# Dividing one 512x512 weight product into halves, once, in a two-block attention kernel

## The chip, the core and the metric

The kernel runs on one NeuronCore of a Trainium2 chip. Its engines run side by side, each with an instruction queue of its own: TensorE (PE; its weight loads are listed apart as PEld), VectorE (DVE), ScalarE (ACT), GpSimd (POOL), and SyncE (SP), which here only issues DMAs. SBUF is the working memory of 128 partitions; PSUM holds what TensorE writes. The metric is the device time of one execution in microseconds, the median of several runs.

## The reference

Eight images of 512 channels and 32x32 pixels (1024 tokens), all in float32, go through two attention blocks. What matters here is block 1:

```
xn = group_norm(x)
q, k, v = q_w @ xn, k_w @ xn, v_w @ xn          # conv1x1, with biases
attn = softmax(q^T k / sqrt(512))
out = attn @ v^T                                # tokens x channels
return x + p_w @ out                            # conv1x1, with a bias
```

Block 0 is of the same kind with eight heads of 64 channels, group norm in 32 groups and an output projection of its own.

In block 1 the attention weights act on tokens and `p_w` on channels, so the value and the output weights can be multiplied with each other first, once for all images: Z = p_w v_w, a 512x512 matrix. The kernel does this, and the same with the query and key weights (M).

## The kernel before

The kernel is written in one function, `two_attention_blocks_kernel`, and a scheduling layer places each engine's instructions; `tc.keep_in_program_order` pins an instruction to its place in the written order. `matmul` and `transpose` (L67, L70) are pinned throughout, so in the profile most TensorE work has one of these two lines. Each float32 matmul of the code is two matmul records and two weight loads in the profile.

A prologue runs once. It makes M (`product(wq, wk, "m")`), runs image 0's value, query and key products for block 0, then makes Z, then a few bias rows. After it comes the loop over images: scores, exponentials and value products of block 0 (`attention0`), the projection, and block 1 of the image before, interleaved with block 0 of the image after.

The large products already use a scheme of seven multiplications of halves in place of eight, with sums and differences of the halves made beforehand (`left_sums`, `right_sums`, `wino`). The two weight products M and Z do not: `product` multiplies 512x512 by 512x512 in 16 matmuls of 128x128 by 128x512, four for each block of 128 rows, and ScalarE copies each finished block from PSUM to SBUF. Two blocks make one pair tile, and SP stores each pair to `products["z"]` in DRAM. `prepare("z")` later reads it back in quarters, and VectorE makes the sums that block 1 uses, from image to image.

What surrounds the product, in the order of the text:

- the last products of block 0's keys for image 0 (`conv(... "k0_0")`, ended by `finish()`). VectorE combines each result at L387; the last L387 is the last thing VectorE does for it
- `keep2("m", t)`: four GpSimd operations (L306) on 128x896 elements in SBUF make further sums of M, and SP stores them (L308)
- `natural(raw_v, "v", "bc")`: 16 transposes of the value weights on TensorE, then four copies from PSUM to SBUF (L776), pinned, shared by VectorE and ScalarE: tile 0's first half on VectorE and second half on ScalarE, tile 1 the same
- `norm1.group_mean`: a tiny matmul of 4 columns, and four tiny VectorE steps (L115 to L121), two of which (L117, L119) read two tensors in SBUF
- `product(wv, raw_p, "z")`: the product of this document. ScalarE copies its blocks at L789, SP stores at L791
- `norm1.affine`: another matmul of 4 columns (tile `gvar`), which feeds VectorE and then four tiny GpSimd steps
- `bias_products`: 12 matmuls of one row, copied by VectorE (L805) and sent through DRAM
- the first scores of `attention0`: TensorE, ScalarE for the exponentials (L621), VectorE for their sums (L623, L625). The next image's tiles, loaded by SP (L209), are scaled on ScalarE (L140) after the first group of exponentials.

SBUF tiles of 128x1024 elements come from one pool of 32 buffers (`big_tile`, `pair_tile`): a new tile waits for the last use of the buffer that it takes. PSUM tiles come from three pools a, b, c of two banks each in the prologue and a pool of two for small results (`acc_tile`).

The product itself and the place that calls it:

```
L789  nc.scalar.copy(ts_[ic // 2][:, ic % 2, :], ps)
...
raw_p0 = raw("p0", 3)
wv = natural(raw_v, "v", "bc")
norm1.group_mean(acc_tile("gmean_0_1")[:, :KC])
product(wv, raw_p, "z")
norm1.affine(acc_tile("gvar_0_1")[:, :KC])
```

Of the kernel before, what the change touches and what calls it, by code (L numbers as in the profile page):

```python
# [9 lines left out]
F32 = mybir.dt.float32  # L10
I32 = mybir.dt.int32
AF = mybir.ActivationFunctionType
ALU = mybir.AluOpType
AX = mybir.AxisListType

P = 128
# [13 lines left out]
def two_attention_blocks_kernel(  # L30
# [8 lines left out]
    nc = tc.nc  # L39
    B, C, T = x.shape  # L40
    KC = C // P
# [24 lines left out]
    def matmul(*args, **kw):  # L66
        tc.keep_in_program_order(nc.tensor.matmul(*args, **kw))  # L67

    def transpose(*args):
        tc.keep_in_program_order(nc.tensor.transpose(*args))  # L70
# [14 lines left out]
    products = {n: dram.tile([C, C], F32, name=f"product_{n}") for n in "mz"}  # L85
# [90 lines left out]
    def main_path(ctx):  # L176
# [8 lines left out]
        def big_tile(name, shape=(P, T)):  # L185
            return big.tile(list(shape), F32, tag="big", name=name)

        def pair_tile(name):
            return big_tile(name, (P, 2, HT))
# [5 lines left out]
        ps_pools = []  # L195
# [11 lines left out]
        def load_x(b, c, what):  # L207
            t = big_tile(f"{what}_{b}_{c}")
            nc.sync.dma_start(t, x[b, c * P : (c + 1) * P, :])  # L209
            return t  # L210
# [543 lines left out]
        def raw(n, i):  # L754
            ts_ = [pair_tile(f"raw{n}_{h}") for h in range(2)]
            for kc in range(KC):
                nc.sync.dma_start(ts_[kc // 2][:, kc % 2, :], w[i, ts(kc, P), :])
            return [ts_[kc // 2][:, kc % 2, :] for kc in range(KC)]

        def ps_tile(n, name):  # L760
            return acc_tile(name) if n == "acc" else ps_pools["abc".index(n)].tile([P, HT], F32, tag="ps", name=name)

        def spread(f, n):

            for i in range(n):
                f(i, nc.scalar.copy if i % 2 else nc.vector.tensor_copy)


        def natural(wt, nm, banks):
            ts_ = [pair_tile(f"nat{nm}_{h}") for h in range(2)]  # L770
            t = [ts_[o // 2][:, o % 2, :] for o in range(KC)]
            pt = [ps_tile(banks[o // 2], f"tr_w{nm}_{o}") for o in range(KC)]
            for kc in range(KC):
                for o in range(KC):
                    transpose(pt[o][:, ts(kc, P)], wt[kc][:, ts(o, P)], ident)
            spread(lambda o, copy: tc.keep_in_program_order(copy(t[o], pt[o])), KC)  # L776
            return t

        def product(lhs, rhs, nm, hooks=()):

            hooks = dict(hooks)
            ts_ = [pair_tile(f"prod{nm}_{h}") for h in range(2)]
            for ic in range(KC):
                ps = ps_tile("a", f"ps_w{nm}_{ic}")
                for kc in range(KC):
                    matmul(ps, lhs[kc][:, ts(ic, P)], rhs[kc], start=(kc == 0), stop=(kc == KC - 1))
                    if ic * KC + kc in hooks:
                        hooks[ic * KC + kc]()
                nc.scalar.copy(ts_[ic // 2][:, ic % 2, :], ps)  # L789
                if ic % 2:  # L790
                    nc.sync.dma_start(  # L791
                        products[nm][ts(ic // 2, C // 2), :].rearrange("(kc p) o -> p kc o", p=P), ts_[ic // 2]
                    )

        def bias_products(lhs):

            n = len(lhs)
            ps = acc_tile("ps_bias")
            for kc in range(KC):
                for i, (m, vec) in enumerate(lhs):  # L800
                    matmul(ps[32 * i : 32 * i + 1, :], pcol(vec, kc), m[kc], start=(kc == 0), stop=(kc == KC - 1))
            row = big_tile("bias_rows")
            rows = dram.tile([n, C], F32, name="bias_rows_dram")
            for i in range(n):
                nc.vector.tensor_copy(row[32 * i : 32 * i + 1, :C], ps[32 * i : 32 * i + 1, :])  # L805
            nc.sync.dma_start(rows, row[0 : 32 * n : 32, :C])
            cols = const.tile([P, n, KC], F32, name="bias_cols")
            for i in range(n):
                nc.sync.dma_start(cols[:, i, :], rows[i].rearrange("(c p) -> p c", p=P))
            return [cols[:, i, :] for i in range(n)]  # L810

        def prologue():
            raw_k = raw("k", 5)
            raw_q = raw("q", 4)
            h0 = [load_x(0, c, "h0") for c in range(KC)]
            first = {n: prepare(n) for n in "vqk"}
            wk = natural(raw_k, "k", ("a", "b"))
            wq = natural(raw_q, "q", ("c", "acc"))
            norm = GroupNorm(0, "0_0", pinned=True)
            for c in range(KC):  # L820
                norm.stats(c, h0[c])
            hf, steps = image_factors(h0, "h0_0")

            def normed():
                norm.affine(acc_tile("gvar_0_0")[:, :KC])
                for c in range(KC):
                    norm.apply(nc.scalar if c % 2 else nc.gpsimd, h0[c], h0[c], c)

            product(
                wq, wk, "m", {6: lambda: norm.group_mean(acc_tile("gmean_0_0")[:, :KC]), 9: normed},  # L830
            )
            raw_v = raw("v", 6)
            raw_p = raw("p", 7)
            for f in first["v"][1]:
                f()
            background.extend(steps)
            for n in "qk":
                background.extend(first[n][1])
            v = by_token(weight_factors(first["v"][0]), hf, "v0_0", middle=(2, 5, 6, 7), back=4)
            finish()  # L840
            run_background(len(background))
            keep("v", first["v"][0])
            x1 = [load_x(1, c, "x1") for c in range(KC)] if B > 1 else []
            norm1 = GroupNorm(0, "0_1")
            background.extend(lambda c=c: norm1.stats(c, x1[c]) for c in range(len(x1)))
            q = conv(weight_factors(first["q"][0]), hf, pcols("bq0"), "q0_0")
            keep2("q", first["q"][0])
            keep2("k", first["k"][0])
            t, steps = prepare("m")
            k = conv(weight_factors(first["k"][0]), hf, pcols("bk0"), "k0_0", hooks=[[], [], [], [], steps])  # L850
            finish()
            keep2("m", t)
            raw_p0 = raw("p0", 3)
            wv = natural(raw_v, "v", "bc")
            norm1.group_mean(acc_tile("gmean_0_1")[:, :KC])
            product(wv, raw_p, "z")
            norm1.affine(acc_tile("gvar_0_1")[:, :KC])
            bias = bias_products([(wk, "bq1"), (raw_p, "bv1"), (raw_p0, "bv0")])
            later = []
            for n in "pz":  # L860
                t, steps = prepare(n)
                later.append(steps)
                later.append([lambda n=n, t=t: keep(n, t), load_weight])
            later.append([
                lambda: tc.keep_in_program_order(nc.vector.tensor_copy(ubias, bias[0])),
                lambda: tc.keep_in_program_order(nc.vector.tensor_add(obias[1], bias[1], pcols("bp1"))),
                lambda: tc.keep_in_program_order(nc.vector.tensor_add(obias[0], bias[2], pcols("bp0"))),
                load_weight,
            ])
            return v, q, k, norm1, later  # L870

        psum_pools("first", 2)
        v, q, k, norm0, later = prologue()
# [121 lines left out]
        for b in range(B):  # L995
# [4 lines left out]
            h, loads, applies = [], [], []  # L1000
            if b > 0:
                h, loads, applies = begun(load_again, norm1, b - 1, "h1")
            elif B > 1:
                h, loads, applies = begun(load_x, norm0, 1, "h0")
# [4 lines left out]
            a = channel_tiles(f"a0_{b}")  # L1009
# [4 lines left out]
            if b > 0:  # L1014
                hf, t = image_factors(h, f"h1_{b - 1}", here)
                for i, fs in enumerate((t[:1], t[1:2], (t[2], t[4]), (t[6], t[3]), (t[5], t[7]), steps[:2], steps[2:4])):
                    extra[2 * i + 3] += fs
            elif B > 1:
                hf, t = image_factors(h, "h0_1", here)
# [9 lines left out]
            if b > 0:  # L1029
# [6 lines left out]
                _, _, mean, affine = norm_hooks(norm1, f"1_{b}")  # L1036
                if b + 1 < B:
                    h, loads, applies = begun(load_x, norm0, b + 1, "h0")
                else:
                    h, loads, applies = begun(load_again, norm1, b, "h1")  # L1040
                ahead = [loads, *([f] for f in applies)]
                layer1_rest(b - 1, inner, gf, gsteps, stats, [[], mean, [], affine], ahead)
                if b + 1 < B:
                    hf, steps = image_factors(h, f"h0_{b + 1}")
                    background.extend(steps)
                    v, f, norm0 = values(b + 1, hf)
                    q, k = keys_and_queries(b + 1, f, norm0, ())
            elif B > 1:
                v, f, norm0 = values(1, hf, [[], [], [], [], [*steps[:7], scaled, steps[7]]])
# [3 lines left out]
                q, k = keys_and_queries(1, f, norm0, hooks)  # L1053
            else:
# [8 lines left out]
                h, loads, applies = begun(load_again, norm1, 0, "h1")  # L1063
# [20 lines left out]
        ps = acc_tile("ps_good")  # L1084
# [183 lines left out]
```

## Time and profile before

| | |
|---|---|
| median of 3 runs | 2849.69 us (2848.17 to 2850.7) |
| the profiled execution's own time | 2849.52 us |
| its span, first to last instruction | 2847.7 us |
| mean granted TensorE clock | 0.999 |
| prologue, up to the first scores | 0 to 120.7 us |
| the product Z on TensorE | 103.17 to 116.98 us |
| GpSimd's four sums of M (L306) | 98.02 to 106.34 us |
| store of Z's first and second half issued on SP | 114.24 and 122.54 us |
| load of image 1's first tile issued; its first use on ScalarE | 123.91; 134.70 us |

The profile is of one execution. A line of a timeline has the start, the length, the engine, the line of the code, the operation, the tile written and the tiles read, the shapes and how many instructions in a row are drawn together; in brackets stands how long the engine was idle before it and what ended the wait. A line of a tile or a source line has three lengths of one instruction in ns (shortest, median, longest), and the first and last start. Lengths of matmuls are modelled and overlap: the distance between two starts is what one costs when many follow each other.

### The profile page before, as it was taken

The page shows a single profiled execution, that of the slowest core. Times are in us where ns is not written, and L with a number is a line of the kernel's source. Part 1 is how long each engine was busy: PE and PEld are TensorE (multiplying, and loading weights), DVE is VectorE, ACT ScalarE, POOL GpSimd, SP SyncE. Part 2 cuts the span into 40 slices and gives each one's busy share as a digit, 9 for nine tenths or more (in the row PEclk, how much of TensorE's full clock was granted, in tenths as well). Part 3 has the DMA queues.
Part 4 walks back from the last instruction along what each step waited for, and adds up shares of the span by engine and source line. Part 5 has one row for each costly group of instructions (what it writes and reads, how often), then busy time and mean ns, then how long its engine had stood idle before and what let it go on. Part 6 is the DMA issues. An engine that isn't in the chain of part 4 may idle for free.

```text
span 2847.7 us, 32456 instructions
## 1 busy us (share of the span) xinstructions
PE 2827.0 (99%) x11846; PEld 1690.0 (59%) x11846; DVE 2083.8 (73%) x2733; ACT 929.0 (33%) x1177; POOL 1205.4 (42%) x1193
## 2 busy tenths in 40 slices
PE   9999999999999999999999999999999999999998
PEld 5435635866367653677537674376743868338584
DVE  5587787766877678776787757877578775887765
ACT  1252452214522145220552215422154311633130
POOL 2123215732167321673227722277123761147672
PEclk9999999999999999999999999999999999999999
DMA  8632403133031230322213232122311223012301
GB/s 276 190 127 90 180 20 126 36 144 134 20 144 65 106 128 26 134 94 97 109 49 111 94 118 92 49 108 97 134 72 49 107 101 142 35 52 94 121 2 68
DMA packets 91597, 280.59 MB, mean 99 GB/s; under 512 B 10595, under 2 KB 36387, under 8 KB 82470
## 3 DMA queue, kind: packets, MB, share of 16 engines
q1 hardware_dynamic: 89638, 276.15, 26.7%
q10 hardware_dynamic: 1792, 2.29, 0.2%
q8 instruction: 96, 1.57, 0.2%
q14 instruction: 71, 0.58, 0.1%
HBM read 227.31 MB, written 51.09 MB: 98 GB/s over the span
## 4 chain that ended last, share of the span: by engine, by line
PE 97%; DVE 2%; issue 1%; ACT 0%; POOL 0%; DVEq 0%; POOLq 0%; ACTq 0%
PE sc L67 16%; PE av L67 16%; PE psb_av L67 6%; PE psb L67 5%; PE psa_av L67 4%; PE psc_av L67 4%; PE psc L67 3%; PE psa L67 3%; PE psb_z L67 3%; PE psb_p L67 3%; PE psb_v L67 3%; PE psb_k L67 3%; PE psb_g L67 3%; PE psb_q L67 2%; PE psa_p L67 2%; PE psa_z L67 2%
## 5 line engine op out<-in xcount | busy, mean ns | idle before, releaser
L625 DVE TENSOR_TENSOR sum<-sum,e 128x1024 f32<-128x1024 f32 x384 | 522.4, 1360 | 41.8 <-DVE sum L623 1.4
L621 ACT ACTIVATE e<-sc 128x1024 f32<-128x1024 f32 x512 | 476.8, 1053 | 73.2 <-PE sc L67 72.3
L67 PE MATMUL sc<-q,k 64*128 64x512 f32 x2048 | 458.7, 596 | 0.5
L67 PE MATMUL av<-e,v 128*64 128x512 f32 x2048 | 453.6, 596 | 0.0
L67 PEld LDWEIGHTS sc<-q,k 64*128 64x128 f32 x2048 | 193.3, 186 | 239.2 <-ACT e L621 104.0
L67 PEld LDWEIGHTS av<-e,v 128*64 128x64 f32 x2048 | 141.4, 137 | 304.3 <-issue 304.3
L588 POOL TENSOR_TENSOR all_recs<-all_recs,rc 128x256 f32<-128x256 f32 x72 | 65.2, 905 | 528.3 <-DVE rc L586 520.7
L644 POOL TENSOR_TENSOR a<-a,r 128x512 f32<-128x512 f32 x56 | 112.6, 2010 | 265.0 <-DMA r<-rows 220.8
L586 DVE RECIPROCAL rc<-sums 128x256 f32<-128x256 f32 x72 | 126.4, 1756 | 46.4 <-PE sums L67 26.5
L532 POOL TENSOR_TENSOR k<-k,k 128x256 f32<-128x256 f32 x28 | 20.0, 727 | 315.8 <-DVE u_k L527 315.8
L639 ACT COPY a<-av 128x512 f32<-128x512 f32 x64 | 37.4, 585 | 318.2 <-PE av L67 318.2
L623 DVE TENSOR_TENSOR sum<-e,e 128x1024 f32<-128x1024 f32 x64 | 78.5, 1226 | 58.9 <-ACT e L621 58.9
L67 PE MATMUL psb<-inner,inner_h 128*128 128x256 f32 x448 | 116.1, 382 | 1.2 <-DVE u L671 0.5
L67 PE MATMUL psa_av<-e,z 128*128 128x512 f32 x256 | 113.3, 596 | 0.0
L140 ACT ACTIVATE h<-h,b,s 128x1024 f32<-128x1024 f32 x62 | 78.4, 1268 | 93.9 <-DMA h<-in_x 77.3
L411 POOL TENSOR_TENSOR inner_h<-h,inner_h 128x256 f32<-128x256 f32 x120 | 106.8, 892 | 2.2
L67 PEld LDWEIGHTS psb<-inner,inner_h 128*128 128x128 f32 x448 | 83.9, 190 | 16.9 <-POOL inner L426 3.8
L411 POOL TENSOR_TENSOR inner_h<-h 128x256 f32<-128x256 f32 x60 | 58.8, 979 | 78.5 <-ACT h L140 78.5
L685 POOL TENSOR_TENSOR sum<-sum,e 128x1024 f32<-128x1024 f32 x32 | 76.2, 2380 | 27.5 <-ACT e L681 26.2
L67 PE MATMUL psb_g<-inner_h,w_m 128*128 128x256 f32 x336 | 86.0, 383 | 0.3
L411 POOL TENSOR_TENSOR inner_h<-t_h 128x256 f32<-128x256 f32 x90 | 77.9, 868 | 10.8 <-PE psc_av L67 9.5
L67 PEld LDWEIGHTS psa_av<-e,z 128*128 128x128 f32 x256 | 48.0, 190 | 57.2 <-issue 56.6
(344 smaller groups left out, 5535.4 us busy)
## 6 DMA issues: line engine op xcount, KB each, us to landing
x<-in_x SPq DMA_DIRECT2D x36, 512.0 KB
h<-in_x SPq DMA_DIRECT2D x32, 512.0 KB
spill<-x SPq DMA_DIRECT2D x32, 512.0 KB
h<-spill SPq DMA_DIRECT2D x32, 512.0 KB
x<-spill SPq DMA_DIRECT2D x32, 512.0 KB
out<-x SPq DMA_DIRECT2D x64, 256.0 KB
w_p<-sums_p SPq DMA_DIRECT2D x8, 1792.0 KB
r<-rows SPq DMA_DIRECT2D x112, 128.0 KB
```

What stands on the lines that cost most here:

```text
L67: tc.keep_in_program_order(nc.tensor.matmul(*args, **kw))
L140: tc.keep_in_program_order(nc.scalar.activation(dst, src, AF.Identity, bias=b, scale=s))
L411: pin(nc.gpsimd.tensor_tensor(dst, x, y, ALU.subtract))
L532: nc.gpsimd.tensor_tensor(d, x, y, ALU.add)
L586: nc.vector.reciprocal(rc, sums)
L588: nc.gpsimd.tensor_tensor(all_recs, all_recs, rc, ALU.add)
L621: nc.scalar.activation(e, sc, AF.Exp, scale=(C // 8) ** -0.5)
L623: nc.vector.tensor_add(total, es[0], e)
L625: nc.vector.tensor_add(total, total, e)
L639: nc.scalar.copy(dst, av)
L644: nc.gpsimd.tensor_tensor(dst, dst, r, ALU.mult)
L685: on = lambda dst, x, y: lambda: tc.keep_in_program_order(nc.gpsimd.tensor_tensor(dst, x, y, ALU.add))
```

## The change

Z is made in halves, by seven products of 256x256 matrices in place of eight. With the operands in quarters (a11, a21, a12, a22 and b11, b12, b21, b22), VectorE makes four sums of each operand; every product is four matmuls of 128x128 by 128x256. PSUM tiles collect products that are added; three partial results are carried from one tile to others by ScalarE copies or VectorE additions. The sums of the right operand are placed ahead of `natural`, those of the left operand behind the tiny steps of the group mean. Only Z is made in this way; M is still made by `product`. `raw` and `natural` now also return their pair tiles.

```diff
         for kc in range(KC):
             nc.sync.dma_start(ts_[kc // 2][:, kc % 2, :], w[i, ts(kc, P), :])
-        return [ts_[kc // 2][:, kc % 2, :] for kc in range(KC)]
+        return [ts_[kc // 2][:, kc % 2, :] for kc in range(KC)], ts_
...
         spread(lambda o, copy: tc.keep_in_program_order(copy(t[o], pt[o])), KC)
-        return t
+        return t, ts_
...
+        def product_in_halves(lhs, right, nm):
+            s1, s2, s3, s4 = (pair_tile(f"half{nm}_{j}")[:, :, : C // 2] for j in range(4))
+            a11, a21, a12, a22 = (lhs[k][:, :, ts(i, C // 2)] for k in range(2) for i in range(2))
+            for dst, x, y, op in (
+                (s1, a21, a22, ALU.add), (s2, s1, a11, ALU.subtract), (s3, a11, a21, ALU.subtract),
+                (s4, a12, s2, ALU.subtract),
+            ):
+                tc.keep_in_program_order(nc.vector.tensor_tensor(dst, x, y, op))
+            left = {1: a11, 2: a12, 3: s4, 4: a22, 5: s1, 6: s2, 7: s3}
+            ts_ = [pair_tile(f"prod{nm}_{h}") for h in range(2)]
+            uc = {w: pair_tile(f"half_{w}{nm}") for w in "uc"}
+            def block(r, cc):
+                return ts_[r][:, :, ts(cc, C // 2)]
+            ps = {}
+            def mm(n, j, start):
+                if start:
+                    ps[n] = ps_pools["abc".index(n)].tile([P, 2, C // 2], F32, tag="ps", name=f"ps_h{nm}_{j}")
+                for i in range(2):
+                    for kc in range(2):
+                        matmul(
+                            ps[n][:, i, :], left[j][:, kc, ts(i, P)], right[j][:, kc, :],
+                            start=start and i == kc == 0, stop=kc == 1, skip_group_check=True,
+                        )
...
+            mm("a", 1, True)
+            ps["b"] = ps_pools[0].tile([P, 2, C // 2], F32, tag="ps", name=f"ps_h{nm}_6")
+            nc.scalar.copy(ps["b"], ps["a"])
+            mm("c", 5, True)
+            nc.scalar.copy(c, ps["c"])
+            mm("a", 2, False)
+            nc.scalar.copy(block(0, 0), ps["a"])
+            mm("b", 6, False)
+            nc.scalar.copy(u, ps["b"])
+            mm("c", 3, False)
+            nc.vector.tensor_add(block(0, 1), ps["c"], u)
+            mm("b", 7, False)
+            nc.vector.tensor_add(block(1, 1), ps["b"], c)
+            store(0)
+            mm("b", 4, False)
+            nc.scalar.copy(block(1, 0), ps["b"])
+            store(1)
...
             keep2("m", t)
-            raw_p0 = raw("p0", 3)
-            wv = natural(raw_v, "v", "bc")
+            raw_p0, _ = raw("p0", 3)
+            t1, t2, t3, t4 = (pair_tile(f"halfp_{j}")[:, :, : C // 2] for j in range(4))
+            b11, b12, b21, b22 = (raw_p_pairs[k][:, :, ts(i, C // 2)] for k in range(2) for i in range(2))
+            for dst, x, y in ((t1, b12, b11), (t2, b22, t1), (t3, b22, b12), (t4, b21, t2)):
+                tc.keep_in_program_order(nc.vector.tensor_tensor(dst, x, y, ALU.subtract))
+            right = {1: b11, 2: b21, 3: b22, 4: t4, 5: t1, 6: t2, 7: t3}
+            wv, wv_pairs = natural(raw_v, "v", "bc")
             norm1.group_mean(acc_tile("gmean_0_1")[:, :KC])
-            product(wv, raw_p, "z")
+            product_in_halves(wv_pairs, right, "z")
             norm1.affine(acc_tile("gvar_0_1")[:, :KC])
```

In the changed file the differences of the right operand stand at L909, the sums of the left operand at L803, the copies and additions that carry partial results at L831 to L844, and the stores at L823. The rest of the diff passes the changed return values of `raw` and `natural` on.

More of the change, by code (lines that the diff above doesn't have):

```diff
@@ L793, in product @@
                     )
+        def product_in_halves(lhs, right, nm):
[21 more added lines that the diff above has]
+                        )
+            store = lambda r: nc.sync.dma_start(
+                products[nm][ts(r, C // 2), :].rearrange("(kc p) o -> p kc o", p=P), ts_[r]
+            )
+            u, c = (uc[w][:, :, : C // 2] for w in "uc")
+            mm("a", 1, True)
[15 more added lines that the diff above has]
+            store(1)
         def bias_products(lhs):
@@ L812, in prologue @@
         def prologue():
-            raw_k = raw("k", 5)
-            raw_q = raw("q", 4)
+            raw_k, _ = raw("k", 5)
+            raw_q, _ = raw("q", 4)
             h0 = [load_x(0, c, "h0") for c in range(KC)]
             first = {n: prepare(n) for n in "vqk"}
-            wk = natural(raw_k, "k", ("a", "b"))
-            wq = natural(raw_q, "q", ("c", "acc"))
+            wk, _ = natural(raw_k, "k", ("a", "b"))
+            wq, _ = natural(raw_q, "q", ("c", "acc"))
             norm = GroupNorm(0, "0_0", pinned=True)
@@ L831, in prologue @@
             )
-            raw_v = raw("v", 6)
-            raw_p = raw("p", 7)
+            raw_v, _ = raw("v", 6)
+            raw_p, raw_p_pairs = raw("p", 7)
             for f in first["v"][1]:
```

## The prediction

> **What bounds the kernel now.** I read the page's busy times first, then the chain of waits for the same engine, then the timeline of 96 to 132 us engine by engine, because the product that changes runs there once.
>
> ```profile
> PE 2827.0 (99%) x11846; PEld 1690.0 (59%) x11846; DVE 2083.8 (73%) x2733; ACT 929.0 (33%) x1177; POOL 1205.4 (42%) x1193
> PE 97%; DVE 2%; issue 1%; ACT 0%; POOL 0%; DVEq 0%; POOLq 0%; ACTq 0%
> ```
>
> TensorE is busy for all but 20.7 us of the span, most of it at the start. Whatever TensorE loses or gains in the prologue therefore moves the end by the same amount; there is almost no later wait to take it up.
>
> ```profile
> 101.03 1.64 PE L70 MATMUL tr_wv<-ident,rawv 128*128 128x128 f32 x13 [0.52 <-DVE k L387]
> 102.50 0.28 PE L67 MATMUL gmean<-mv,gm 128*128 128x4 f32 x2
> 103.17 13.97 PE L67 MATMUL ps_wz<-rawp,natv 128*128 128x512 f32 x32 [0.38 <-ACT natv L776]
> 116.98 0.28 PE L67 MATMUL gvar<-dv,gm 128*128 128x4 f32 x2
> ```
>
> The product holds TensorE from 103.17 to 116.98, 13.81 us: 16 matmuls of the code are 32 records, 0.429 us from one to the next. VectorE and GpSimd beside it:
>
> ```profile
> 100.22 0.75 DVE L387 SCALAR_TENSOR_TENSOR k<-psc_k,par,u_k 128x512 f32<-128x512 f32 x1 [0.97 <-PE psc_k L67]
> 102.37 1.29 DVE L776 COPY natv<-tr_wv 128x512 f32<-128x512 f32 x2 [1.40 <-PE tr_wv L70]
> 103.77 0.56 DVE L117 TENSOR_TENSOR d<-mv,gmean 128x4 f32<-128x4 f32 x1
> 104.36 2.00 DVE L119 TENSOR_TENSOR d<-d 128x4 f32<-128x4 f32 x1
> 106.39 0.16 DVE L121 TENSOR_TENSOR dv<-d,mv 128x4 f32<-128x4 f32 x1
> ```
>
> ```profile
> 98.02 4.25 POOL L306 TENSOR_TENSOR prepare_m<-prepare_m 128x896 f32<-128x896 f32 x2 [23.94 <-DVE prepare_m L286]
> ```
>
> ```profile
> 102.22 4.12 POOL L306 TENSOR_TENSOR prepare_m<-prepare_m 128x896 f32<-128x896 f32 x2
> ```
>
> The line to stop at is L119: 128x4 elements in 2.00 us, where the sister at L121 takes 0.16. GpSimd runs four operations on SBUF from 98.02 to 106.34, 2.08 us each, with borders near 100.1, 102.25, 104.3. L117 ends at 104.33, with the third; L119 at 106.36, with the fourth. Each VectorE operation on two SBUF operands waited out one GpSimd operation. The copies from PSUM (L776, 0.65 each) and L387 (0.75, one SBUF tensor) ran through the same stretch at their usual length.
>
> [...] Who goes next when both queues are full, a later stage of the trace shows:
>
> ```profile
> L728 DVE TENSOR_TENSOR t<-e,e x2: 1212/1755/2298, 548.4 to 550.6; 128x1024 f32<-128x1024 f32 x2
> L728 POOL TENSOR_TENSOR e<-e,e x2: 3263/3298/3334, 550.8 to 554.0; 128x1024 f32<-128x1024 f32 x2
> L728 DVE TENSOR_TENSOR t<-e,t x2: 3364/3368/3372, 551.8 to 555.0; 128x1024 f32<-128x1024 f32 x2
> ```
>
> VectorE's third operation takes 3.37 us although 1.21 is its own length: it waited for a GpSimd operation that was itself waiting when VectorE's second ended. They alternate, one each.
>
> [...]
>
> ```profile
> L70 PE MATMUL tr_wk<-ident,rawk x16: 417/421/475, 3.7 to 7.9; 128*128 128x128 f32 x16
> L70 PE MATMUL tr_wq<-ident,rawq x16: 272/420/422, 8.1 to 10.7; 128*128 128x128 f32 x16
> ```
>
> The same transposes take 0.42 us until shortly before 10.7 and then 0.27, as the transposes at 101 us do. From the last wait there (to 6.33) that is some 4.0 us of slow clock. The column of the granted clock reads 1.00 all through, so only durations show it.
>
> **The change part by part.** The order of both programs shows that outside this product each engine keeps its instructions and their order, save a few DMAs on SP; the buffer waits that differ afterwards name work long done.
>
> 1. *Four differences of the right operand (new L909)* come on VectorE straight behind the last L387, which ends at 100.97, and ahead of the two L776 copies. Each subtracts 128x512 in SBUF; the nearest rows, L286 in the prologue, take 0.63 (1.88 for three). They wait for nothing but each other, so their free price is 2.5 us. [...] Alternating: difference 1 to 102.90; GpSimd's third to 104.98; difference 2 to 105.6; GpSimd's fourth to 107.69; differences 3 and 4 to 108.93. Then the first L776 copy, 0.68, to 109.6. TensorE starts the product at 109.65 instead of 103.17: **+6.48**. Behind those differences queue both copies and the mean's small steps, and the first copy is what TensorE waits for. Bounds: below, no lock (copy ends at 104.1, +1.0)[...]. Above, all differences after all of GpSimd's (end 108.9) is no later. I take the alternation.
>
> 2. *Matmuls.* 7 products of 4 matmuls of 256 columns, 56 records. A layer-0 stage has the form:
>
> ```profile
> 289.65 1.03 PE L67 MATMUL psc_k<-inner_h,w_k 128*128 128x256 f32 x4
> 290.51 1.03 PE L67 MATMUL psb_k<-inner_h,w_k 128*128 128x256 f32 x4
> ```
>
> Four in 0.86, so 0.215 each: 56 are 12.04 for 13.81: **-1.77**. The weight loads (0.19) stay hidden, as they do there.
>
> 3. *Sums of the left operand (L803).* After the copies (to 110.3) and the mean's four small steps at 0.16 to 0.2, VectorE starts them at about 111.0; GpSimd is idle, so 0.63 each: 111.6, 112.3, 112.9, 113.5. Product 5 wants the first. At full clock product 1 would be done at 111.4: +0.3. At half clock product 1 lasts to 113.1 and hides it: 0.
>
> 4. *Bank b.* Product 4 directly follows product 7 on one PSUM tile and must wait until the VectorE addition has read it (0.69, as L375 and L238). Drain and start before it: a 512-column record ends 0.59 after its start while the next may start at 0.43; with about 0.1 for signals this is **+1.0** (bounds 0.7 and 1.2). ScalarE's copies of banks have another product of 1.72 us between and are hidden; if that cover went, each would cost about 0.6.
>
> 5. *Clock.* TensorE has nothing from 102.78 to 109.65, 6.87 us[...]. By the start of this trace 4.0 us at half clock lose **+2.0**[...]; 0 if the clock stays.
>
> 6. *Behind the product.* The variance matmul, the bias rows and the first scores need only TensorE and small operands. ScalarE's last copy (0.59) ends within the 3.7 us of bias matmuls. On SP both product stores come later, the v weights move behind the second store, and the next image's first load moves behind all the reloads of z, from 123.91 to an estimated 133. Before, it landed at 134.70, a little ahead of ScalarE's output copy at 135.85; now that copy stands at 143.6 and the load should land by 138: 0. GpSimd's delayed sums shift the stores of m by 1.4, used hundreds of us later.
>
> Sum: 6.48 - 1.77 + 0 + 1.0 + 2.0 = **+7.7 us**. The profiled execution's own time was 2849.52 (span 2847.7 and 1.8 around it): 2857.2; on the median of 2849.69 it is 2857.4. I take 2857.3.
>
> **The rivals.**
> - *Lock without the cold clock.* For it: other waits of TensorE are under 1 us after the start, so no cooling was ever seen here. [...] 6.48 - 1.77 + 0.3 + 1.0 = +6.0: 2855.6.
> - [...] differences done at 104.75, start at 105.5 (+2.33)[...]: 2.33 - 1.77 + 0.4 + 1.0 = +2.0: 2851.6. Against: L728.
> - *Not slower: no hold-up at all.* The place is the first difference at 100.97. If it ran at once in 0.63, TensorE would start at 104.2 (+1.03), and with the left sums' wait 0.4 the product would end at -0.3, if the hand-over of bank b does not show; 2849.3, or 2850.3 if it does. It decides from a GpSimd operation that does not block. Against: L119.
> - *A late load on top.* The second store took 10.9 us (122.54 to 133.43) before the reload behind it could issue, and the image load 10.8 from issue to use. Both again from an estimated 126.0 with 1.4 of issuing puts the image at 149.1, 5.5 beyond the copy: +13.2, 2862.8. Against: the store now stands ahead of the v weights (1792 KB).
>
> **How the numbers follow.** Forecast 62, no cold clock 18, [...] no hold-up 6, late load 7 in 100. About 0.2% (5.7 us, 2855.4) is what a measurement of this kernel can tell from no change. Slower: 0.58 of the forecast's 0.62 (a short cold stretch with a short hand-over falls below), 0.09 of 0.18, and 0.07: 0.74. Same: 0.24. Faster, by something I do not see: 0.02. The range takes in the cases[...] with room for what they leave uncertain: 2851.5 to 2861.
>
> **What would show it.** Right: L909 in four lengths of about 1.9, 2.7, 2.7 and 0.6 us, two of L306 at 2.7, L776 near 108.9, the first ps_hz near 109.65 with records of some 0.55 us that turn into 0.38[...], a hole of 1.0 between ps_hz's products 7 and 4, the variance matmul near 124.7, and then the same distance to before down to the end. Wrong: L909 at 0.6 throughout, records of 0.38 from the first, or a new wait of ScalarE on the image load.

## The result and the profile after

| | before | after |
|---|---|---|
| median, 20 runs of each | 2849.1 us (2848.02 to 2851.02) | 2853.66 us (2851.43 to 2855.2) |
| the profiled execution's own time; its span | 2849.52; 2847.7 us | 2855.2; 2853.4 us |
| the product on TensorE | 103.17 to 116.98 us | 109.58 to 124.47 us |
| first scores after the first value-weight transpose | 20.70 us | 27.70 us |

The changed kernel takes 1.0016 times as long (95% interval 1.001 to 1.0021), 4.6 us more. The forecast said 7.7 more. The profiled execution of after is the longest of its 20, so I profiled the kernel a second time below.

The page of after, busy times and chain of waits:

```profile
PE 2826.9 (99%) x11870; PEld 1694.7 (59%) x11870; DVE 2092.2 (73%) x2743; ACT 930.1 (33%) x1178; POOL 1201.7 (42%) x1193
PE 97%; DVE 2%; issue 0%; DMA 0%; POOL 0%; ACT 0%; SPq 0%; DVEq 0%
```

TensorE has 24 records more and is busy for 0.1 us less. Its idle time grew from 20.7 to 26.5 us. The timelines of after, engine by engine, tell where:

```profile
103.01 0.28 PE L67 MATMUL gmean<-mv,gm 128*128 128x4 f32 x2
109.58 3.65 PE L67 MATMUL ps_hz<-rawp,natv 128*128 128x256 f32 x8 [6.29 <-issue]
113.06 1.89 PE L67 MATMUL ps_hz<-halfp,halfz 128*128 128x256 f32 x8
...
119.97 1.89 PE L67 MATMUL ps_hz<-halfp,halfz 128*128 128x256 f32 x8
122.64 1.99 PE L67 MATMUL ps_hz<-halfp,natv 128*128 128x256 f32 x8 [0.78 <-DVE prodz L841]
124.47 0.28 PE L67 MATMUL gvar<-dv,gm 128*128 128x4 f32 x2
```

```profile
101.39 1.93 DVE L909 TENSOR_TENSOR halfp<-rawp 128x512 f32<-128x512 f32 x1
103.35 2.44 DVE L909 TENSOR_TENSOR halfp<-rawp,halfp 128x512 f32<-128x512 f32 x1
105.72 2.55 DVE L909 TENSOR_TENSOR halfp<-rawp,rawp 128x512 f32<-128x512 f32 x1
108.20 0.68 DVE L909 TENSOR_TENSOR halfp<-rawp,halfp 128x512 f32<-128x512 f32 x1
108.80 1.27 DVE L776 COPY natv<-tr_wv 128x512 f32<-128x512 f32 x2
```

```profile
98.53 9.20 POOL L306 TENSOR_TENSOR prepare_m<-prepare_m 128x896 f32<-128x896 f32 x4 [23.89 <-DVE prepare_m L286]
```

The fourth L909 gives the length of a difference that meets nobody: 0.68 us. The three ahead of it, on tiles of the same shape, run into GpSimd's operations and take 1.93, 2.44 and 2.55. GpSimd's four lost only 0.9 us together (9.20; before 8.32, from 98.02 to 106.34): two of them took 2.52 us in place of 2.08. TensorE's bracket says "issue" for its 6.29 us because no semaphore event stands next to the start; the copy at 108.80, queued behind the four differences, tells what it waited for. Then the first product takes 3.48 us (109.58 to 113.06) and the next 1.73, for the same eight records. In a narrow window the granted clock shows why; the columns of this view are the window, its length, the busy time of each engine, the clock, the DMA share and the GB/s:

```profile
core 0: us, PE busy (x) PEld busy (x) DVE busy (x) ACT busy (x) POOL busy (x), PEclk, DMA share, GB/s
102.90:109.58 6.68, 0.39 (x6) 0.33 (x4) 6.65 (x6) 1.07 (x2) 4.83 (x2) 0.74 0.30 95
109.58:113.06 3.48, 3.48 (x9) 2.83 (x9) 3.34 (x9) 0.00 (x0) 0.00 (x0) 0.51 0.95 281
113.06:119.97 6.91, 6.91 (x34) 6.08 (x33) 0.21 (x1) 2.33 (x4) 0.00 (x0) 1.00 0.86 250
```

The clock is 0.51 in the first product and 1.00 after it. The page's 40 slices average this away.

### The profile page after: what moved, and what is told of

The parts are those of the page before. It is cut to its first block, busy times and chain, and to the rows that moved or that the text cites. A ratio compares the mean times of both kernels' runs of the same rounds, so it can differ in the third digit from the quotient of the medians.

```text
span 2853.4 us, 32517 instructions
## 1 busy us (share of the span) xinstructions
PE 2826.9 (99%) x11870; PEld 1694.7 (59%) x11870; DVE 2092.2 (73%) x2743; ACT 930.1 (33%) x1178; POOL 1201.7 (42%) x1193
## 4 chain that ended last, share of the span: by engine, by line
PE 97%; DVE 2%; issue 0%; DMA 0%; POOL 0%; ACT 0%; SPq 0%; DVEq 0%
PE sc L67 16%; PE av L67 16%; PE psb_av L67 5%; PE psb L67 5%; PE psa_av L67 4%; PE psc_av L67 4%; PE psc L67 3%; PE psa L67 3%; PE psb_z L67 3%; PE psb_p L67 3%; PE psb_v L67 3%; PE psb_k L67 3%; PE psb_g L67 3%; PE psb_q L67 2%; PE psa_p L67 2%; PE psa_z L67 2%
## 5 line engine op out<-in xcount | busy, mean ns | idle before, releaser
L625 DVE TENSOR_TENSOR sum<-sum,e 128x1024 f32<-128x1024 f32 x384 | 519.6, 1353 | 42.1 <-DVE sum L625 1.4
L681 ACT ACTIVATE e<-e 128x1024 f32<-128x1024 f32 x64 | 65.8, 1053 | 48.6 <-DVE e L671 26.2
```

The source lines that it names most:

```text
L625: nc.vector.tensor_add(total, total, e)
L681: nc.scalar.activation(e[c, cc, r], e[c, cc, r], AF.Exp, scale=scale)
```

## The experiments

Two theories stood at the start. By *lock* the prediction and the expectations mean that a VectorE operation on two SBUF tensors waits out GpSimd operations, as the three long L909 do (1.93 to 2.55 us in place of 0.68), by *cold clock* the 0.51 of the first product. *Lock and clock:* all that the change does lies between the transposes and the first scores, as forecast; the missing 3 us are given back elsewhere. *Halves:* the halved product itself brings something further on, through other stores or another timing of z. Each trace is cut in three, so that a program can be compared piece by piece. *First scores* is their start, counted from the first value-weight transpose (what lies ahead of that differs by up to 1.8 us between executions, and by 1.3 between two of one kernel). *Later waits* is the stretch from there to `ps_good`, the program's last matmul, which tests the reciprocals of the softmax. *End* is from `ps_good` to the last instruction. The times are against the kernel before as it ran beside each; all else is of one profiled execution each, first scores and later waits as differences to the trace before.

| kernel | median less that of before, us | ratio (95%) | first scores | later waits | end |
|---|---|---|---|---|---|
| before | | | 0 | 0 | 9.24 |
| after | +4.6 | 1.0016 (1.001 to 1.0021) | +7.00 | -0.06 | 7.50 |
| e1, after again | +4.5 | 1.0016 (1.001 to 1.0023) | +7.46 | -2.15 | 7.40 |
| e2, differences early | -0.1 | 0.9997 (0.9989 to 1.0006) | +1.76 | -2.15 | 7.34 |
| e3, early, other order | -4.0 | 0.9985 (0.9979 to 0.9992) | -0.78 | -1.32 | 7.41 |
| e4, hole filled | +2.3 | 1.0008 (1.0 to 1.0016) | +5.45 | -1.10 | 7.35 |
| e5, before again | +0.5 | 1.0001 (0.9993 to 1.001) | +0.01 | +0.08 | 9.58 |
| e6, differences alone | +6.9 | 1.0024 (1.0015 to 1.0033) | +7.94 | -1.58 | 9.59 |
| e7, GpSimd reads nothing | -2.5 | 0.9991 (0.9983 to 1.0) | +0.56 | -2.61 | 7.11 |
| e8, before, 12 small matmuls | +1.5 | 1.0004 (0.9996 to 1.0013) | +2.17 | -1.66 | 7.54 |
| e9, before, 7 large matmuls | +2.2 | 1.0009 (1.0 to 1.0018) | +5.50 | -1.89 | 7.48 |
| e10, before, 28 on VectorE | -1.3 | 0.9998 (0.9988 to 1.0008) | +0.01 | -1.00 | 9.70 |
| e11, before, 2 small matmuls | -2.2 | 0.9992 (0.9982 to 1.0002) | +0.06 | -0.10 | 7.04 |
| e12, e11 again | -1.6 | 0.9994 (0.9985 to 1.0002) | +0.05 | +1.20 | 7.48 |

**The changed kernel again.** No edit.

> The changed kernel itself once more, in new executions. Theory[...]: the four L909 differences again take about 1.9, 2.4, 2.5 and 0.7 us and the first ps_hz stands 6.2 to 6.6 us behind the transposes' end. If the cold clock comes in every execution, ps_hz's first product takes 3.4 to 3.7 us again[...]. Time: 4 to 5 us over the kernel before, as measured.

The hole is the same 6.3 us, and the slow clock lasts a little longer, into product 5:

```profile
108.31:111.86 3.55, 3.55 (x9) 2.83 (x10) 3.41 (x9) 0.00 (x0) 0.00 (x0) 0.50 0.95 282
111.86:113.97 2.11, 2.11 (x9) 1.81 (x8) 0.14 (x1) 0.57 (x1) 0.00 (x0) 0.82 0.91 248
```

What the prologue loses is steady (7.0 and 7.5); what comes after it is not: 2.1 us of later waits separate two executions of one program. One profile is not enough to judge that stretch.

**The differences made early.** In the last key product, where GpSimd is idle (from 73.8 us to 97.7):

```diff
-k = conv(weight_factors(first["k"][0]), ..., hooks=[[], [], [], [], steps])
+k = conv(weight_factors(first["k"][0]), ..., hooks=[[], [], differences, [], steps])
...
-for dst, x, y in ((t1, b12, b11), (t2, b22, t1), (t3, b22, b12), (t4, b21, t2)):
-    tc.keep_in_program_order(nc.vector.tensor_tensor(dst, x, y, ALU.subtract))
```

> Only the place of the four differences of the right operand is changed: they are made in the middle of the last key product, about 85 us, when GpSimd is idle. Theory: each takes 0.6 to 0.7 us, the copies from the transposes come at 102.4 again and the product starts at about 103.2 at full clock. What is left is the wait of product 5 for the first left sum, because the group mean's two small steps still wait for GpSimd until 106.4 (about +2.3), the hand-over of bank b (+1.0) and the matmuls (-1.8): +1 to +2 us on the kernel before, so some 3 to 6 us less than the changed kernel. Rival (the sums cost what they cost wherever they stand, or the loss arises behind the product): still +4 to +7.

The four take 0.68 to 0.69 us there, from 83.4 us on, and the hole is gone. First scores are +1.76, as expected; that the time is -0.1 and not +1 to +2 comes from the two later columns, to which the last experiments turn. More is not won in the prologue, because another operation of VectorE on two SBUF tensors now makes TensorE wait. VectorE's timeline of e2, first the differences:

```profile
83.41 0.68 DVE L905 TENSOR_TENSOR halfp<-rawp 128x512 f32<-128x512 f32 x1
...
85.34 0.68 DVE L905 TENSOR_TENSOR halfp<-rawp,halfp 128x512 f32<-128x512 f32 x1
...
103.46 0.57 DVE L117 TENSOR_TENSOR d<-mv,gmean 128x4 f32<-128x4 f32 x1
104.07 2.00 DVE L119 TENSOR_TENSOR d<-d 128x4 f32<-128x4 f32 x1
106.09 0.16 DVE L121 TENSOR_TENSOR dv<-d,mv 128x4 f32<-128x4 f32 x1
106.17 0.68 DVE L803 TENSOR_TENSOR halfz<-natv,natv 128x512 f32<-128x512 f32 x1
```

and TensorE's:

```profile
102.86 1.96 PE L67 MATMUL ps_hz<-rawp,natv 128*128 128x256 f32 x8 [0.38 <-ACT natv L776]
106.91 1.99 PE L67 MATMUL ps_hz<-halfp,halfz 128*128 128x256 f32 x8 [2.09 <-DVE halfz L803]
```

The small step at L119 waits out a GpSimd operation as in before (2.00 us; 0.16 in after, where GpSimd is done by then), but now the left sums stand behind them and product 5 behind these.

**Early, the left sums first, another order of products.** On top of e2, the group mean's steps go behind the left sums, and no two products in a row use one bank with a VectorE addition between:

```diff
-            norm1.group_mean(acc_tile("gmean_0_1")[:, :KC])
-            product_in_halves(wv_pairs, right, "z")
+            product_in_halves(wv_pairs, right, "z", lambda: norm1.group_mean(acc_tile("gmean_0_1")[:, :KC]))
...
             nc.scalar.copy(c, ps["c"])
-            mm("a", 2, False)
-            nc.scalar.copy(block(0, 0), ps["a"])
+            between()
             mm("b", 6, False)
             nc.scalar.copy(u, ps["b"])
-            mm("c", 3, False)
-            nc.vector.tensor_add(block(0, 1), ps["c"], u)
+            mm("a", 2, False)
+            nc.scalar.copy(block(0, 0), ps["a"])
             mm("b", 7, False)
             nc.vector.tensor_add(block(1, 1), ps["b"], c)
+            mm("c", 3, False)
+            nc.vector.tensor_add(block(0, 1), ps["c"], u)
```

> As the one before, and two more edits: the left sums are placed ahead of the group mean's small steps, and the products run in the order 1 5 6 2 7 3 4, so that no product follows another on the same bank. Theory: no hole of 1 us ahead of product 4; the first left sum at about 104.9, the second one behind GpSimd's last operation at 107.7, for which product 6 waits about 1 us; product from 103.2 to about 116.4: -0.6 us on the kernel before (-1.7 if the left sums are not held up by GpSimd). Rival (the loss arises behind the product): +3 or more.

TensorE's timeline of e3:

```profile
104.30 1.93 PE L67 MATMUL ps_hz<-halfp,halfz 128*128 128x256 f32 x8
106.06 0.28 PE L67 MATMUL gmean<-mv,gm 128*128 128x4 f32 x2
106.81 1.97 PE L67 MATMUL ps_hz<-halfp,halfz 128*128 128x256 f32 x8 [0.46 <-DVE halfz L803]
...
113.79 1.89 PE L67 MATMUL ps_hz<-halfp,natv 128*128 128x256 f32 x8
115.52 0.28 PE L67 MATMUL gvar<-dv,gm 128*128 128x4 f32 x2
```

No wait stands at the last product any more, and the 0.46 us ahead of product 6 are what GpSimd's work still costs: the second left sum takes 2.45 us from 104.21 on, the two behind it, with GpSimd done at 106.12, 0.68 each. The kernel is 4.0 us faster than the one before, the best of all. Only 0.78 of it is won by the first scores, though.

**The hole filled.** The changed kernel with unused matmuls ahead of the product, so that TensorE has no idle stretch:

```diff
+            fill = acc_tile("fill")
+            for _ in range(7):
+                matmul(fill, ident, raw_p[0], start=True, stop=True)
             product_in_halves(wv_pairs, right, "z")
```

> The changed kernel with seven extra 128x512 matmuls, whose result nobody reads, put on TensorE between the group mean and the product, where it would idle; nothing else is changed. They take 6.0 us of the 6.3 us hole. Theory: the product starts where it did (109.6, at most 0.3 later) and its first product takes 1.8 us in place of 3.5, so the scores start about 1.6 us earlier than in the changed kernel. In the time this is 1.6 us less if every execution of the changed kernel has the cold stretch, and 0 to 0.8 if only some have. Rival (the long first records are the wait for operands, not the clock): 3.5 us again.

Clock by window:

```profile
108.28:110.08 1.80, 1.80 (x9) 1.44 (x9) 1.66 (x7) 0.00 (x0) 0.00 (x0) 1.00 0.93 278
```

The first product takes 1.80 us at clock 1.00, and first scores come 1.55 and 2.0 us earlier than in the two traces of after; the times differ by 2.2. So the slow clock costs 1.6 to 2.2 us, and the idle stretch is its cause.

**The kernel before again.** No edit; it shows how far one kernel differs from itself.

> The kernel before, once more. The changed kernel's profiles put the scores 7.0 to 7.5 us later, counted from the transposes, but its time is only 4.5 us longer, and the one profile of before ends 6.9 us after its last store is issued where five profiles of changed programs end 5.1 us after it. Theory A: the end of the program before is longer by 1.8 us in every execution: 6.9 again. Theory B: that was chance, as are the waits of about 0.8 us between: 5.1, and another early part. Time: no change (within 0.1%).

Its end is long again, 9.58 us, as theory A has it, and its later waits are the same to 0.08 us. Two of them stand out in both traces of before: in block 1's value product TensorE waits for an addition of VectorE (L238), and ahead of a sum of exponentials for VectorE's part of it (L625). TensorE's waits in the trace before (total, times, longest):

```profile
PE psb_av L67 <- DVE w_av L238: 0.8, 1, 0.8
PE sums L67 <- DVE sum L625: 0.7, 1, 0.7
```

**The differences alone.** The four differences as in the change, but the product undivided:

```diff
-            product_in_halves(wv_pairs, right, "z")
+            product(wv, raw_p, "z")
```

> The old product of 16 matmuls, with only the four differences of the right operand made ahead of it (their result is not used). Theory: the lock alone; L909 in four lengths of about 1.9, 2.4, 2.5 and 0.7 us, product from 6.0 to 6.6 us later with about 1.7 us of cold clock at its start: scores 7.7 to 8.3 later, counted from the transposes, so 0.5 to 1 us later than in the changed kernel. Rival (the halves themselves bring the loss): 2.5 us or less.

TensorE's timeline of e6:

```profile
109.77 15.99 PE L67 MATMUL ps_wz<-rawp,natv 128*128 128x512 f32 x32 [6.30 <-issue]
125.60 0.28 PE L67 MATMUL gvar<-dv,gm 128*128 128x4 f32 x2
```

The hole is the differences' alone, and the undivided product too takes 15.83 us in place of 13.81: 2.0 for the slow clock. Three traces can now be cut where the granted clock itself changes. From the start of the product to the return of the clock, in after, e1 and e6 (TensorE's busy time alone, then the clock, the DMA share and the GB/s):

```profile
109.58:112.99 3.41, 3.41 (x8) 0.50 0.94 280
108.31:112.63 4.32, 4.32 (x10) 0.50 0.94 284
109.77:113.85 4.08, 4.08 (x5) 0.50 0.95 284
```

In each of them the clock stood at 0.50 for 6.8 us, from 106.16, 105.81 and 107.02 us on, so part of that fell into the idle stretch. Half of what was left when the product began, 1.7, 2.2 and 2.0 us, is the loss that the products show (1.75, 2.20 and 2.02). This is why two executions of one program lose different amounts.

Later waits fall by 1.58 without any halves, so the halves are not needed for it. The end does not fall.

**GpSimd without reads.** GpSimd's four sums of M become settings that read nothing; block 1's scores are computed without these sums, of the same shapes:

```diff
-                tc.keep_in_program_order(nc.gpsimd.tensor_tensor(dst, x, y, op))
+                tc.keep_in_program_order(
+                    nc.gpsimd.memset(dst, 0.0) if n == "m" else nc.gpsimd.tensor_tensor(dst, x, y, op)
+                )
```

> The changed kernel, but GpSimd's four operations on M's halves (L306) are four fills with zero into the same tiles: they write SBUF and read nothing. Block 1's scores are made without those sums. VectorE's order is untouched. Theory[...]: the four L909 take 0.7 us each although GpSimd is busy, L776 comes at about 103.5, the product starts about 1 us later than in the kernel before and at full clock, and the scores stand about +0.5 to +1 us, counted from the transposes. Rival (the place in VectorE's queue[...]): lengths of 1.9 to 2.5 as before and 6 us or more.

VectorE's timeline of e7, where the differences have line L911:

```profile
100.77 0.68 DVE L911 TENSOR_TENSOR halfp<-rawp 128x512 f32<-128x512 f32 x1
101.49 0.69 DVE L911 TENSOR_TENSOR halfp<-rawp,halfp 128x512 f32<-128x512 f32 x1
102.10 0.69 DVE L911 TENSOR_TENSOR halfp<-rawp,rawp 128x512 f32<-128x512 f32 x1
102.70 0.69 DVE L911 TENSOR_TENSOR halfp<-rawp,halfp 128x512 f32<-128x512 f32 x1
```

Where they took 7.60 us together they now take 2.75, at the same place in VectorE's queue and on tiles of the same shape. So it was GpSimd's work beside them, not the place. The edit did more than was meant, though: the fills wait for nothing that VectorE makes, and GpSimd ran them 20 us earlier:

```profile
79.53 3.20 POOL L307 MEMSET prepare_m<- 128x896 f32 x4 [5.54 <-PE psc_q L67]
```

While the differences ran, from 100.77 us on, GpSimd was idle, and the expected "although GpSimd is busy" did not come about. The fills and the differences never ran at the same time, so whether GpSimd's reads or any of its work on SBUF held VectorE up stays open.

**What the missing microseconds follow.** After these seven the prologue was settled; the end (7.1 to 7.5 us with the halves, 9.2 to 9.6 without) and the later waits were not. Two kernels add unused matmuls to the kernel before, in the manner of e4: 12 of 4 columns, which bring its number of records to that of after, and 7 of 512 columns, a delay of 6 us.

> The kernel before with 12 unused matmuls of 4 columns (24 records, the number by which the halved product exceeds the whole one) ahead of the product. They cost about 0.14 each: the first scores come 2.5 to 3.5 us later. End of the program, from the first matmul of the last output projection (ps_good) to the last instruction: 9.2 to 9.6 us in every trace with the product undivided, 7.1 to 7.5 in every one with the halves. Theory A, the end follows the number or the place of TensorE's instructions: 7.1 to 7.5 here, and the time up by no more than 1. Theory B, it belongs to the halved product itself: 9.2 to 9.6 here, and the time up by about the delay less what later waits give back (0 to 2).

> The kernel before with 7 unused matmuls of 512 columns (14 records, 6.0 us) ahead of the product, which is otherwise as before. First scores 5.5 to 6.5 us later. Theory A, later waits of TensorE give back 1 to 2 us whenever the loop over images starts some us later, whatever made it late: from the first scores to the last output projection 1 to 2.2 us less than before, and the time up by about 4 to 5. Theory B, they give it back only where the product is halved or GpSimd meets VectorE: no change there (0 +- 0.2), and the time up by 6. The end, from the last projection on: 9.2 to 9.6 if it belongs to the undivided product, 7.1 to 7.5 if any shift does it.

Both have the short end (7.54 and 7.48) with the product undivided: the end isn't the halves'. Both lose 1.7 to 1.9 us of later waits, e9 as its theory A says. The delay of e8 is 2.17 us, less than the 2.5 to 3.5 expected. For e9 A had the time up by 4 to 5; it is 2.2, since the end is shorter too. For e8 the time doesn't fit as well: +1.5 where A allowed 1. Its runs scatter over 4.2 us (2847.38 to 2851.55) and the profiled one is the shortest, so its row shows the good case.

Next, 28 instructions more on VectorE against 8 more on TensorE (4 records, 4 loads):

```diff
+            scr = const.tile([P, 4], F32, name="scr")
+            for _ in range(28):
+                tc.keep_in_program_order(nc.vector.memset(scr, 0.0))
```

> The kernel before with 28 unused settings of 4 columns on VectorE behind the product (VectorE is idle there), 28 instructions more in all, as many as the delayed product's 7 unused matmuls added on TensorE. First scores as before. From ps_good to the end of the program: 9.2 to 9.6 us if TensorE's own number of instructions decides, 7.1 to 7.6 if the number of all the program's instructions does.

> The kernel before with 2 unused matmuls of 4 columns (4 records and 4 loads) ahead of the product: 0.3 us, first scores at most 0.6 later. From ps_good to the end: 7.1 to 7.6 if a few instructions of TensorE are enough, 9.2 to 9.6 if it takes more than these 8. Later waits: as before if the kernel needs more than half a microsecond of shift to lose them (0 +- 0.3 from the first scores to ps_good), 1 to 2 us less if any shift does it.

The span and TensorE's last matmul in the timeline, first of e10, then of e11:

```profile
core 0 of [0], span 2846.1 us
...
2836.40 0.19 PE L67 MATMUL ps_good<-ones,both 128*1 128x1 f32 x2
```

```profile
core 0 of [0], span 2844.9 us
...
2837.86 0.19 PE L67 MATMUL ps_good<-ones,both 128*1 128x1 f32 x2
```

9.70 us with the VectorE instructions, 7.04 with two unused matmuls. So it is an addition to TensorE's own instructions that shortens the end, and 8 are enough. The lines of TensorE's instruction queue (PEldq) show where. The program ends with a jump over a second path (L1224 in before, L1227 in e11) and a last meeting of all engines (L1264, L1267). First before, then e11:

```profile
L1224 PEldq EVENT_SEMAPHORE  x1: 51/51/51, 2843.6 to 2843.6; - x1
L1264 PEldq DRAIN  x2: 8/8/8, 2847.0 to 2847.3; - x2
```

```profile
L1227 PEldq EVENT_SEMAPHORE  x1: 51/51/51, 2842.9 to 2842.9; - x1
L1267 PEldq DRAIN  x2: 8/8/8, 2843.1 to 2844.5; - x2
```

In before, TensorE comes to the meeting at 2847.0, 3.4 us behind its semaphore step at the jump, and all the others are there by 2845.1. In e11 it comes under 0.2 us behind that step. In all four traces with the long end this stretch of TensorE's queue lasts 3.2 to 3.8 us, in all ten with the short end 0.15. e11 once more, in more runs:

> The kernel before with 2 unused matmuls of 4 columns, again and in more runs. If the shorter end is real and steady: from ps_good to the end 7.0 to 7.6 us, and the median 1.5 to 2.5 us under the kernel before (ratio 0.9992, with an interval that leaves 1 out). If the first look was chance: the end at 9.2 to 9.7, or the median within 0.7 of before.

The end is 7.48 and the median 1.6 lower, but the interval reaches 1.0002, so it does not leave out 1 as expected. Its later waits are 1.2 us longer than in the trace before with nothing shifted: again this stretch differs by execution.

## Why the prediction was right and where it was off

1. *The four differences: right.* Forecast lengths were 1.9, 2.7, 2.7 and 0.6; measured 1.93, 2.44, 2.55, 0.68. The forecast counted the first to the end of GpSimd's second operation at 102.27 and let the two engines take turns from there. The product started at 109.58; 0.5 us of that was already there at the last L387, so the step cost 5.91 where the forecast had 6.48: two of the waits were 0.15 and 0.26 shorter than taken. e2 and e7 show GpSimd's operations at that moment as the cause, since in both the differences meet none and take 0.68 to 0.69. What it is that the two engines share isn't shown. The rival at 2851.6, in which the differences run one behind another from 102.27 on, falls with the lengths, "no hold-up" with the hole.
2. *The matmuls: right.* A product takes 1.73 us at full clock, 0.216 per record.
3. *Left sums hidden: right.* They start at 110.65 and the first is done before product 5 at 113.06. At full clock (e4) product 5 came 0.07 later than it could.
4. *Bank b: right.* Products 7 and 4 start 2.67 us apart (119.97, 122.64), 0.94 over a product's 1.73, where the forecast had 1.0; the addition between them (L841) takes 0.69 from 121.89 on, and product 4 starts 0.06 after its end. e3 has no such hole.
5. *Clock: right.* The first product takes 1.75 us too long in one trace; in the other 1.82, and product 5 adds 0.38. e6 gives 2.0, e4 1.55 and 2.0 against the two traces of after. That an idle stretch would bring the slow clock, and that it would be half, was the author's estimate: the trace of before shows only slow transposes at its start, 0.42 us in place of 0.27. The clock of 0.50 behind holes of 6.3 us, and its absence in e4, were measured afterwards. "Lock without the cold clock" falls with the 0.51. Steps 1 to 5 were forecast at +7.7 together and came to +7.0 and +7.5 at the first scores.
6. *Behind the product: the step that failed.* The late load did not come: ScalarE's use of the image at 138.54 stands 3.9 us ahead of the copy at 142.42. But the forecast's 0 for what lies behind the product, and "then the same distance to before down to the end", are wrong. So is the opening sentence that there is "almost no later wait to take it up": TensorE's waits between the first scores and `ps_good` add up to 4.5 us in the trace before (2717.74 us, 2713.20 of them busy). Two terms were missing. The end is shorter by 1.7 to 2.2 us (9.24 and 9.58 in two traces of before, 7.50 and 7.40 in two of after), because TensorE has more instructions (shown by e8, e9, e11 and e12 against e10 and e6). And the loop over images loses later waits: 0.06 and 2.15 us in the two traces of after. Counted against the trace before, with the first, +7.0 becomes +5.2; with both, +7.5 becomes +3.5. The measured +4.6 lies between. The forecast time, 2857.3 us, was 3.6 too high: 0.2 to 0.7 of it by steps 1 to 5, about 2.4 to 2.9 by this one, and the last 0.6 because the median of before is that much lower in 20 runs than in the 3 it started from.

The later waits are not settled as well. In nine traces whose first scores moved by more than half a microsecond they changed by -2.61 to -0.06, 1.6 us less on average; in the five that did not move (before and e5, e10 to e12) by -1.00 to +1.20, on average 0.0. Most of it is the two waits shown under e5: together 1.5 us in before, after, e5 and e11, 2.5 in e12, 0.8 to 1.2 in e3, e4 and e10, and 0 to 0.4 in the six that lost most. The medians do not bear out so much. When the change of the first scores and of the end (against 9.41, the mean of the two traces of before) is taken off each median's difference, the nine are left with -0.6 on average (-1.4 to +1.2), after and e1 with -0.5 and -1.0, and e5 and e10 to e12 with -0.2. e6 and e9 show that no halves are needed for it. Whether a shift shortens these waits in every execution, and why, isn't shown.

Nor is it shown what holds TensorE up at the end. The kernel reads a flag into registers there and jumps over a second path. The DMA view has seven reads of instructions in the last stretch in e10 and e11 alike, and I did not try to move the jump.

## What to carry to other kernels

Before adding VectorE work on two SBUF operands, look at what GpSimd has queued at that moment: the cost was not 4 times 0.68 but nearly 6 us on the path, and the same four instructions some 18 us earlier left no hole. Here a wait of TensorE of 6.3 us was paid with about 2 more in the products behind it, in three traces of three. And when a change of a few microseconds is judged, add instructions that do nothing, to see what the program gives or takes for any change at all: here two unused matmuls lowered the median by 1.6 to 2.2 us (with intervals that just reach no change), about half of what the best version gained.

## What the runs showed of the hardware that was not expected

- The end of the program took 9.2 to 9.7 us in four traces with TensorE's instructions as before, and 7.0 to 7.5 in ten with at least 8 more of them. The difference lies in TensorE's own instruction queue behind the jump (3.2 to 3.8 us against 0.15).
- VectorE and GpSimd took turns, but the sides did not lose alike: three differences waited 1.25, 1.76 and 1.87 us (less 0.68 for their own work), 4.9 together, while two of GpSimd's operations grew by 0.44 each.
- The granted clock of a narrow window shows the slowed TensorE (0.51, 0.50) that the mean of the span, 0.998, hides. The view prints 1.00 at the program's start too, where the transposes take 0.42 us in place of 0.27; but the trace of before has its first entry for the clock at 10.08 us, so the 1.00 ahead of it is no reading.
- The slow stretch had the same length, 6.8 us, in three traces. What differed was how much of it had gone by when TensorE's work came back (2.5 to 3.4 us), and with it the loss.
